# Edge-gated graph layer on one core: other steps for the pieces of rows and lists

## The chip, the core and the metric

One core of a Trainium2 chip runs one launch. The metric is device time in microseconds. The core has a matrix engine (TensorE; PE in the profile, its weight loads PEld), VectorE (DVE), ScalarE (ACT), GpSimd (POOL) and a queue that only issues transfers (SP). ACT and POOL issue transfers too, each in the order of its own program.

## The reference

With B = 16, N = 1024 nodes and D = 256, `adj` has about nine entries other than zero in a column, 24 at most being handled in the main part:

```python
pre_u = einsum('bud,dk->buk', h, W1[:d])
pre_v = einsum('bvd,dk->bvk', h, W1[d:])
hidden = relu(pre_u[:, :, None, :] + pre_v[:, None, :, :] + b1)
S = sigmoid(einsum('buvk,ko->buvo', hidden, W2)[..., 0] + b2[0])
a = einsum('buv,bud->bvd', S * adj, h)
m = einsum('uv,bud->bvd', adj, h) * h
z = beta1 * h + beta2 * (a @ Wa + ba) + beta3 * (m @ Wm + bm)
```

Only edges (u, v) with adj[u, v] other than zero count, so the kernel visits edges and never forms the full `hidden`.

## The kernel before

The batches are four groups g of four, and the nodes v eight tiles vt of 128. A block is one (g, vt); there are 32, in the list `order` (lines 365 to 367): g = 0 and 1 for vt 0 to 5, then vt 6 and 7 of both, then g = 2 and 3. A block has T = 10 steps, each with 128 edges. The main loop (line 684 on) makes 320 steps n, with s = n mod 10, and all engines run their instructions in the order in which the loop writes them: nothing reorders them.

In step n:
- `aggregate(n-1)` (line 560): PE sums the neighbours' rows of the step before, weighted, into `acc`.
- `fetch_val` (line 341) and `fetch(n+4)` (line 453) on POOL: up to two small gathers of edge values, then the gather of 128 rows of `table[g]` into one of five `fetched` buffers, free once it was aggregated.
- `gate(n)`: DVE adds the gathered row to `pc` (line 539) and makes four weighted sums (line 543); ACT makes the sigmoid (546) and the weights `left` (549).
- `left_adj(n+1)` (533), and every fifth step `load_mark` (516), on ACT.
- `do(n)`: DVE work that an earlier step put off.
- `expand(n+2)` (523): PE makes the next `pc`, of which there are two buffers.

A block's own work lies at fixed s. `halves` of the next block (418 to 425) has two PE products at s = 0 and 2, each put in X by ACT and into `low` by DVE one step later (419), and ACT copies at 3, 4 and 6. `turn_over` (578 transposes, 581 ACT copy of LT, 591 DVE `times_h` a step later) stands at s = 1, twice at 7, and at 9. `block_end` (608) stands at s = 3, 4, 5, 6, with DVE's sum into `h_blk` (612) at s = 5 and 7 and the output on SP.

Two kinds of work are cut into pieces and put between, at the end of a step:
- Rows: `rows(k)` makes the left half of a table tile, x W1[:d], in two halves: PE product (384), ACT copy into `tab` (400), and a step after the second half the write to the table on SP (403). `load_hT` on SP (373) brings the transposed x, `copy_h` on ACT's queue (378) copies x itself into the right half of the table. `plan` gives for each tile the step of its load and of its two halves.
- Lists: `lists(vt)` (from line 236) finds the edges of a tile in ten pieces: 1 load of the key on POOL; 2 key (244 DVE, 245 ACT); 3 maxima (251); 4 `cut` and the sorted tops (254 to 266); 5 prefix sums on PE (270); 6 `held` (275 to 285), which reads the PE result; 7 mark (288 to 300, `few` on ACT 298); 8 four transfers of `whose` (304, on ACT's queue for vt from 4), the products of line 307 and the ACT copy `L` (311); 9 indices (315 to 326), which also hands ten value gathers to `fetch_val`, two a step; 10 `onehot` (331). `advance` says in which steps the pieces of lists 4 to 7 stand: an offset each from n = 0, 20, 50 and 80.

`halves`, `rows`, `turn_over`, `block_end` and the PE results of lists from vt = 3 on share the two PSUM buffers `misc`; a new use takes a buffer once its last reader is done.

Before the loop stands an opening, `script`: 16 row halves ("r") for all eight tiles of g = 0, lists 0 to 3 (digits), the first block's `halves` ("h"), list 0's values ("v") and five fetches ("f"). Behind it come `load_mark(0)`, two expands and `left_adj(0)`.

Of the kernel before, what the change touches and what calls it, by code (L numbers as in the profile page):

```python
# [17 lines left out]
def kernel(  # L18
# [44 lines left out]
    NT = N // P  # L63
# [166 lines left out]
    EARLY = 4  # L230
# [200 lines left out]
    def do(step):  # L431
        for f in due.pop(step, ()):
            f()
# [12 lines left out]
    def where(n):  # L446
        k, s = divmod(n, T)
        w, j = divmod(s, TW)
        return k, *order[k], w, j
# [9 lines left out]
    made = [lists(vt) for vt in range(NT)]  # L459
    turn = [(g, vt) for g in range(2) for vt in (*range(FIRST, NT), *range(FIRST))]  # L460
# [8 lines left out]
    for i in range(COPIES):  # L469
        copy_h(turn[i], nc.sync)  # L470

    script = ("r 0 0", "r r 0", "r 1", "0 r 1 1", "0 0 r r", "1 r 0 2 2", "r r 0 0 v 2", "1 1 r r",
              "2 r 1 r", "2 2 r r 1 1 h", "2 h 3 3", "2 2 h 3", "f h h 3", "3 3")
    m = 0
    piece = None
    parts = halves(0)
# [21 lines left out]
            else:  # L498
                next(made[int(c)], None)
    do(len(script) - 100)  # L500

    def scale_late():
        nc.vector.tensor_scalar(ba_b, ba_b, be2, None, ALU.mult)
        nc.vector.scalar_tensor_tensor(bias, bias, be3, ba_b, ALU.mult, ALU.add)
        spread(bias_p, bias)
        nc.vector.tensor_scalar(w_a, w_a, be2, None, ALU.mult)
        nc.vector.tensor_scalar(w_m, w_m, be3, None, ALU.mult)
# [10 lines left out]
    def expand(n):  # L518
        k, g, vt, w, j = where(n)
        pcs[n] = psc.tile([P, GD], FP, name="pc")  # L520
        for h in range(2):
            c = slice(2 * h * D, (2 * h + 2) * D)
            nc.tensor.matmul(pcs[n][:, c], marks[n // TW][:, j * P:(j + 1) * P], cuts[k][:, w, c],  # L523
                             start=True, stop=True)


    def left_adj(n):
        k, g, vt, w, j = where(n)
        i = vt * NW + w
        m = len(QUARTERS[j])  # L530
        o = max(2 * j - 1, 0)
        lefts[n] = wk.tile([P, 2, GB, 2, V], FP, name="left")
        nc.scalar.activation(lefts[n][:, :m, :, 0, :], onehot[:, i, o:o + m, :].unsqueeze(2).to_broadcast([P, m, GB, V]),  # L533
                             AF.Copy, scale=val[:, i, j:j + 1])
# [123 lines left out]

    advance = {0: (3,), 2: (3,), 4: (3,)}
    for i, n in zip(range(EARLY, NT), (0, 20, 50, 80)):  # L660
        for o in (0, 4, 5, 6, 7, 9, 11, 13, 15, 17):
            advance[n + o] = (*advance.get(n + o, ()), i)
    loads, at = {}, {}

    def plan(blocks, ns):

        for k, (load, *pieces) in zip(blocks, ns):
            loads[load] = k
            at.update((n, k) for n in pieces)

    plan(turn[NT:], ((0, 5, 8), (6, 12, 15), (12, 18, 22), (17, 25, 28), (24, 32, 35), (31, 38, 42), (38, 45, 48),
                     (43, 50, 52)))
    plan([(2, vt) for vt in range(NT)], ((62 + 10 * i, 68 + 10 * i, 73 + 10 * i) for i in range(NT)))
    plan([(3, vt) for vt in range(NT)], ((146, 152, 157), (156, 162, 167), *((153 + 10 * i, 158 + 10 * i, 161 + 10 * i)
                                                                             for i in range(2, NT))))
    plan(again, ((103,), (113,), (125,), (133,)))
    begun = set(turn[:NT])
# [2 lines left out]
    for n in range(2):  # L680
        expand(n)
    left_adj(0)
    total = BS * T
    for n in range(total + 2):
        k, s = divmod(n, T)
# [25 lines left out]
        if s == 4 and k < BS:  # L711
            hbs[k] = big.tile([P, GB, D], FP, name="h_blk")
            if k < BS - 1:
                g, vt = order[k]
# [55 lines left out]
    with tc.If(any_left > 0):  # L770
        with ExitStack() as s2:
# [3 lines left out]
            for vt in range(NT):  # L775
# [17 lines left out]
                f = fb.tile([P, 2 * GD], FP, name="fb_f")  # L793
# [83 lines left out]
```

## Time and profile before

| | us |
|---|---|
| median of 4 runs | 1203.81 (1197.35 to 1208.98) |
| the profiled execution | 1200.31 |
| its span, first to last instruction | 1198.5 |
| start of the first line-539 add (step 0) | 68.69 |
| VectorE busy | 1067.3 |
| PE busy, PEld busy | 1100.2, 725.7 |
| ScalarE busy | 841.1 |
| mean granted TensorE clock | 0.966 |

A row of the timeline has the start, the length, the engine, the line, the operation, what it writes and reads, and in brackets how long its engine stood idle before it and what ended that. A row of the table by stretches has the stretch, its length, each engine's busy time with its number of instructions, the granted clock as a share of full speed, the transfers' share and their rate. A row of the waits has the time in all, how often, and the longest.

### The profile page before, as it was taken

Reading aid. Unit: us, or ns where it says so; the run is one execution under the profiler, and the core shown is the slowest. Engines: PE = TensorE matmul, PEld = TensorE weight load, DVE = VectorE, ACT = ScalarE, POOL = GpSimd, SP = SyncE. Lnnn points to the kernel's source line nnn. Section 1 sums busy time; section 2 is a strip of 40 time slices with the busy share of each in tenths; the row PEclk is TensorE's granted clock in tenths of the full one; section 3 lists DMA queues with packets and bytes.
Section 4 is the critical chain, followed back from the end, with each engine's and each line's share of the span. In section 5 each row is a group of like instructions: output and inputs, shape, how many; then the busy total and the mean of one; then the engine's idle time right before and its main releaser. Section 6 shows DMA issues by size and latency. Waiting matters only on the chain. (4 is left out here: it accounts for less than half of the span.)

```text
span 1198.5 us, 23788 instructions
## 1 busy us (share of the span) xinstructions
PE 1100.2 (92%) x7633; PEld 725.7 (61%) x7633; DVE 1067.3 (89%) x3515; ACT 841.1 (70%) x2498; POOL 426.6 (36%) x428
## 2 busy tenths in 40 slices
PE   7667988999899898999999999999999999999986
PEld 6544655666556565666566666666666666666653
DVE  8769879979989987999899999999999999999994
ACT  3346666677667765787677777877877777777873
POOL 1647652433253226323233333333323333333330
PEclk9867999999899999999999999999999999999999
DMA  9996899899979978999999999999999999999992
GB/s 289 293 315 225 285 321 323 315 324 383 318 251 351 364 252 296 372 374 360 353 325 375 376 321 374 368 355 383 366 362 346 350 322 330 329 338 327 336 339 80
DMA packets 147046, 391.39 MB, mean 327 GB/s; under 512 B 16752, under 2 KB 105328, under 8 KB 110704
## 3 DMA queue, kind: packets, MB, share of 16 engines
q0 software_dynamic: 50016, 300.50, 68.0%
q1 hardware_dynamic: 81616, 74.99, 19.5%
q10 hardware_dynamic: 15280, 14.29, 3.7%
q8 instruction: 63, 1.03, 0.3%
q14 instruction: 71, 0.58, 0.1%
HBM read 393.78 MB, written 50.33 MB: 371 GB/s over the span
## 5 line engine op out<-in xcount | busy, mean ns | idle before, releaser
L453 POOL DMA_INDIRECT fetched<-table,uidx x320 | 329.8, 1031 | 677.0 <-PE acc L560 490.3
L543 DVE SCALAR_TENSOR_TENSOR t<-t,w_b 128x256 f32<-128x256 f32 x1280 | 469.7, 423 | 20.1 <-DVE t L539 0.5
L539 DVE TENSOR_TENSOR t<-fetched,pc 128x1024 f32<-128x1024 f32 x320 | 389.2, 1216 | 23.2 <-DMA fetched<-table,uidx 9.7
L560 PE MATMUL acc<-fetched,left 128*32 128x256 f32 x4096 | 331.7, 394 | 29.2 <-ACT left L549 19.4
L549 ACT ACTIVATE left<-left,gt 128x32 f32<-128x32 f32 (+1 forms) x1280 | 299.4, 305 | 10.4
L523 PE MATMUL pc<-X,mark 128*128 128x512 f32 x640 | 238.7, 455 | 19.3 <-DVE t L539 10.6
L560 PEld LDWEIGHTS acc<-fetched,left 128*32 128x32 f32 x4096 | 127.5, 110 | 174.3 <-issue 49.1
L523 PEld LDWEIGHTS pc<-X,mark 128*128 128x128 f32 x640 | 97.6, 192 | 155.2 <-issue 104.5
L546 ACT ACTIVATE gt<-sc,b_b 128x4 f32<-128x4 f32 x320 | 95.4, 298 | 135.0 <-DVE t L543 128.4
L608 PE MATMUL misc<-w_a,LT 128*128 128x256 f32 x496 | 127.3, 379 | 0.0
L608 PE MATMUL misc<-w_m,LT 128*128 128x256 f32 x496 | 127.1, 378 | 0.0
L384 PE MATMUL misc<-w_u,hT 128*128 128x256 f32 x448 | 111.2, 396 | 14.1 <-issue 5.8
L533 ACT ACTIVATE left<-onehot,val 128x128 f32<-128x128 bf16 (+1 forms) x320 | 116.6, 365 | 0.0
L384 PE MATMUL misc<-w_v,hT 128*128 128x256 f32 x448 | 108.7, 386 | 0.0
L543 DVE DVE_READ_ACCUMULATOR t<-t,w_b 128x1 f32 x1280 | 105.3, 82 | 0.0
L384 PEld LDWEIGHTS misc<-w_u,hT 128*128 128x128 f32 x448 | 86.7, 197 | 30.3 <-issue 6.8
L608 PEld LDWEIGHTS misc<-w_m,LT 128*128 128x128 f32 x496 | 93.7, 189 | 17.2
L608 PEld LDWEIGHTS misc<-w_a,LT 128*128 128x128 f32 x496 | 94.2, 190 | 12.8
L568 ACT COPY ev<-acc 128x512 f32<-128x512 f32 x128 | 75.2, 587 | 37.0 <-PE acc L560 29.9
L384 PEld LDWEIGHTS misc<-w_v,hT 128*128 128x128 f32 x448 | 87.3, 195 | 14.6
L341 POOL DMA_INDIRECT val<-in_adjT_dram,vidx x80 | 83.9, 1049 | 33.5 <-issue 20.8
L581 ACT COPY LT<-misc 128x512 f32<-128x512 f32 x128 | 71.1, 576 | 21.5 <-PE misc L578 7.1
(158 smaller groups left out, 834.9 us busy)
## 6 DMA issues: line engine op xcount, KB each, us to landing
h_blk<-in_x_dram SPq DMA_DIRECT2D x31, 512.0 KB
out_dram<-h_blk SPq DMA_DIRECT2D x31, 512.0 KB
hT<-in_xT_dram SPq DMA_DIRECT2D x28, 512.0 KB
table<-tab SPq DMA_DIRECT2D x26, 512.0 KB
table<-in_x_dram ACTq DMA_DIRECT2D x24, 512.0 KB
fetched<-table,uidx POOLq DMA_INDIRECT x320
table<-in_x_dram SPq DMA_DIRECT2D x8, 512.0 KB
table<-fetched SPq DMA_DIRECT2D x6, 512.0 KB
```

The lines of the kernel that those rows point to most:

```text
L341: nc.gpsimd.indirect_dma_start(out=val[:, i, j:j + 1], out_offset=None, in_=adj_flat, in_offset=bass.IndirectOffsetOnAxis(ap=vidx[:, i, j: ...
L384: nc.tensor.matmul(p[:, bb * D:(bb + 1) * D], hT[:, 2 * h + bb, i, :], wt[:, i, :], start=(i == 0 and not begun), stop=(i == DC - 1), skip ...
L453: nc.gpsimd.indirect_dma_start(out=fetched[n % NF], out_offset=None, in_=table[g], in_offset=bass.IndirectOffsetOnAxis(ap=uidx[:, vt * NW ...
L523: nc.tensor.matmul(pcs[n][:, c], marks[n // TW][:, j * P:(j + 1) * P], cuts[k][:, w, c], start=True, stop=True)
L533: nc.scalar.activation(lefts[n][:, :m, :, 0, :], onehot[:, i, o:o + m, :].unsqueeze(2).to_broadcast([P, m, GB, V]), AF.Copy, scale=val[:, ...
L539: nc.vector.tensor_tensor(t, fetched[n % NF][:, :GD].rearrange("p (b d) -> p b d", b=GB), pcs.pop(n).rearrange("p (b d) -> p b d", b=GB), ...
L543: nc.vector.scalar_tensor_tensor(t[:, b, :], t[:, b, :], 0.0, w2_b, ALU.max, ALU.mult, accum_out=sc[:, b:b + 1])
L546: nc.scalar.activation(gt, sc, AF.Sigmoid, bias=b2_b)
L549: nc.scalar.activation(lefts[n][:, :m, b, 1, :], lefts[n][:, :m, b, 0, :], AF.Copy, scale=gt[:, b:b + 1])
L560: nc.tensor.matmul(accs[h][b * 2 * V:(b + 1) * 2 * V, r, :], left[:, i, b].rearrange("p k v -> p (k v)"), f[:, GD + b * D:GD + (b + 1) * D ...
L568: nc.scalar.copy(evs[q], accs.pop(q))
L608: nc.tensor.matmul(pz[:, bb * D:(bb + 1) * D], LTs[k][:, c, 2 * h + bb, i, :], wt[:, c, :], start=False, stop=(i == 1 and c == DC - 1), sk ...
```

## The change

The order and the steps of the pieces change; none is added or taken away, and what is computed is the same.

- In the opening, some row halves go in front of list pieces, and list 3's pieces 6 and 7 move from the script's end to behind the two expands and `left_adj(0)`.
- The row pieces of tiles g = 1 go to s = 7, 8, 9 and 1 (from 0, 2, 5 and 8); those of g = 2 to 8 and 1 (from 8 and 3), and the first two tiles of g = 3 likewise (from 2 and 7), with loads up to 4 steps earlier and one a step later.
- The ten pieces of lists 4 to 7 go to s = 0, 4, 6, 9, 1, 4, 6, 7, 9, 0 (from 0, 4, 5, 6, 7, 9, 1, 3, 5, 7).

```diff
-    script = ("r 0 0", "r r 0", "r 1", "0 r 1 1", "0 0 r r", "1 r 0 2 2", "r r 0 0 v 2", "1 1 r r",
-              "2 r 1 r", "2 2 r r 1 1 h", "2 h 3 3", "2 2 h 3", "f h h 3", "3 3")
+    script = ("r 0 0", "r r 0", "r 1", "0 r 1 1", "0 r r 0", "1 r 0 2 2", "r r 0 0 v 2", "r r 1 1",
+              "2 1 r r", "2 r r 2 1 1 h", "2 h 3 3", "2 2 h 3", "f h h 3")
...
     for i, n in zip(range(EARLY, NT), (0, 20, 50, 80)):
-        for o in (0, 4, 5, 6, 7, 9, 11, 13, 15, 17):
+        for o in (0, 4, 6, 9, 11, 14, 16, 17, 19, 20):
             advance[n + o] = (*advance.get(n + o, ()), i)
...
-    plan(turn[NT:], ((0, 5, 8), (6, 12, 15), (12, 18, 22), (17, 25, 28), (24, 32, 35), (31, 38, 42), (38, 45, 48),
-                     (43, 50, 52)))
-    plan([(2, vt) for vt in range(NT)], ((62 + 10 * i, 68 + 10 * i, 73 + 10 * i) for i in range(NT)))
-    plan([(3, vt) for vt in range(NT)], ((146, 152, 157), (156, 162, 167), *((153 + 10 * i, 158 + 10 * i, 161 + 10 * i)
+    plan(turn[NT:], ((0, 7, 8), (3, 9, 11), (11, 18, 19), (15, 21, 28), (23, 29, 31), (32, 38, 39), (35, 41, 47),
+                     (42, 48, 49)))
+    plan([(2, vt) for vt in range(NT)], ((62 + 10 * i, 68 + 10 * i, 71 + 10 * i) for i in range(NT)))
+    plan([(3, vt) for vt in range(NT)], ((142, 148, 151), (152, 158, 161), *((153 + 10 * i, 158 + 10 * i, 161 + 10 * i)
...
     left_adj(0)
+    for _ in range(2):
+        next(made[EARLY - 1])
```

## The prediction

> **What bounds the kernel now.** I read the page's first two parts, then the busy time by stretches of whole blocks, then VectorE's waits, and then the timeline around each long wait. I count in steps: step n begins at the start of the n-th line-539 add in the timeline, s = n mod 10.
>
> ```profile
> span 1198.5 us, 23788 instructions
> PE 1100.2 (92%) x7633; PEld 725.7 (61%) x7633; DVE 1067.3 (89%) x3515; ACT 841.1 (70%) x2498; POOL 426.6 (36%) x428
> PEclk9867999999899999999999999999999999999999
> ```
>
> DVE is the engine with the least rest (1067.3 of 1198.5 us); PE's 92% counts pipelined matmuls whose weight loads take only 61%.
>
> ```profile
> core 0: us, PE busy (x) PEld busy (x) DVE busy (x) ACT busy (x) POOL busy (x), PEclk, DMA share, GB/s
> 68.70:238.00 169.30, 148.10 (x954) 98.03 (x953) 146.43 (x497) 105.33 (x311) 89.54 (x87) 0.91 0.85 290
> 238.00:274.80 36.80, 34.11 (x237) 22.94 (x235) 30.46 (x97) 26.36 (x80) 14.52 (x15) 0.95 0.93 338
> 274.80:354.10 79.30, 70.87 (x480) 46.32 (x477) 71.16 (x242) 52.79 (x158) 29.79 (x29) 0.94 0.92 322
> 354.10:386.70 32.60, 32.27 (x233) 21.38 (x231) 30.32 (x97) 25.82 (x78) 12.34 (x13) 1.00 0.89 318
> 386.70:469.20 82.50, 72.36 (x474) 47.80 (x478) 71.15 (x242) 53.52 (x159) 29.44 (x29) 0.94 0.88 316
> 469.20:704.50 235.30, 227.86 (x1617) 149.68 (x1608) 212.70 (x675) 178.81 (x538) 74.97 (x73) 0.99 0.97 353
> 736.50:931.30 194.80, 191.25 (x1389) 125.51 (x1388) 181.91 (x576) 153.64 (x462) 62.17 (x61) 1.00 0.98 361
> 931.30:1149.10 217.80, 209.77 (x1515) 133.09 (x1513) 210.89 (x673) 172.07 (x526) 71.77 (x71) 1.00 0.93 334
> ```
>
> The rows are blocks 0-3, 4, 5-6, 7, 8-9, 10-16, 18-23 and 24-30. The last seven have no pieces: 31.1 us each with DVE busy 30.1, the floor. A list adds 71.15 - 2 x 30.12 = 10.9 us of DVE work wherever it stands. What lies above floor plus list work is stall: blocks 0-3 18.9 us (169.3 - 124.4 - 26.0 of lists), block 4 5.7, 5-6 6.2, 7 1.5, 8-9 9.4, 10-16 17.6, together 59.3. Blocks 18-23 already have their row pieces at s = 8 and s = 1, as the change puts the others, and stall 8.2, or 1.37 a block.
>
> ```profile
> DVE low L419 <- ACT X L418: 19.6, 14, 4.6
> DVE h_blk L612 <- PE misc L608: 18.8, 22, 2.7
> DVE LT L591 <- ACT LT L581: 15.8, 11, 3.7
> DVE t L539 <- DMA fetched<-table,uidx: 9.7, 17, 1.5
> DVE made L288 <- PE misc L384: 5.7, 1, 5.7
> ```
>
> DVE waits for PE, straight or through an ACT copy: PE is late, not short of time. Most of the second line is s = 5, where the block's end (PE work at s = 3 to 6) is added to h_blk.
>
> **The change, part by part.**
>
> *Opening.* The timeline there:
>
> ```profile
> 37.76 0.72 ACT L298 CAST few<-made 128x640 uint8<-128x640 f32 x1 [5.98 <-issue]
> 39.02 3.68 PE L384 MATMUL misc<-w_u,hT 128*128 128x256 f32 x8 [3.63 <-issue]
> 45.90 0.55 DVE L288 TENSOR_SCALAR made<-upto,R 128x640 f32<-128x640 f32 x1 [5.69 <-PE misc L384]
> 66.03 0.72 ACT L298 CAST few<-made 128x640 uint8<-128x640 f32 x1 [7.02 <-DVE made L292]
> 68.69 1.22 DVE L539 TENSOR_TENSOR t<-fetched,pc 128x1024 f32<-128x1024 f32 x1 [2.04 <-PE pc L523]
> ```
>
> ACT holds row copies behind `few`, which waits for a list's mark on DVE; PE, with both `misc` buffers uncopied, stands 3.63 us. Behind PE, DVE waits 5.69 us for `made`. After the change the copies go first, but PE's matmul on list 1's mark is now ahead of four row halves and itself waits for that mark (ready at 38.4, PE free at 35.4), so some 2.9 of the 3.63 stay. I take 0.7, and the like gap of 0.85 that PE has at 24.6 for list 0: 1.5, less 0.2 for one copy more behind `few`. The last: list 3's held and mark pieces now stand behind the first expands, so ACT's mark cast and PE's L523 run under DVE's work, and the 2.04 before the first add go. Sum -3.3; bounds -1 (the table's DMAs set the end of the opening) and -5.
>
> *Row pieces.* None is added or removed: eight matmul instructions (1.9 us of PE, an estimate from their 0.21 us spacing and the gaps), one ACT copy (0.59) each. By the weight loads in the timeline, PE's own work in a step is about 1.2 us at s = 8, 1.5 at 1, 1.7 at 9, 2.1 at 7, against 2.7 to 3.1 at 0 and 2 to 6. At s = 3 or 5 a piece made L612 wait:
>
> ```profile
> 373.64 0.75 DVE L612 SCALAR_TENSOR_TENSOR h_blk<-h_blk,be,misc 128x512 f32<-128x512 f32 x1 [1.30 <-PE misc L608]
> 749.03 0.69 DVE L419 TENSOR_TENSOR low<-misc,X 128x512 fp32r<-128x512 f32 x1 [0.45 <-ACT X L418]
> 755.42 0.75 DVE L612 SCALAR_TENSOR_TENSOR h_blk<-h_blk,be,misc 128x512 f32<-128x512 f32 x1 [0.25 <-PE misc L608]
> ```
>
> The first is step 75 (piece at 73); the others are steps 183 and 185 (piece at 181): 1.30 becomes 0.70. Blocks 10-16: 17.6 becomes 7 x 1.37 plus the 3.1 us that step 131 waits for the transposed x of a reloaded block, which nothing here moves: 12.7, so -4.9. Bounds 0 (transfers fill what is freed) and -8. Blocks 4 and 7: the L612 and L591 gaps at 42, 45, 47 and 75 (0.41, 0.55, 1.15, 1.30) go; 41 and 71 pay 0.70 each, and pieces at 48 and 49 give PE 1.2 + 1.7 + 3.0 and 3.8 for the two, 9.7 us in steps 48 to 50 against DVE's 8.9, so step 51's `low` comes an estimated 0.8 late: -3.4 + 1.4 + 0.8 = -1.2. The issues move too. SP's loads of hT come up to 4 steps earlier (one a step later) and its table writes up to 6; table 1's last write is at step 50 instead of 53, its first fetch at 56. ACT's copy issues (0.57) move with the loads, into steps without an ACT queue wait in the rows. I cost these at nothing; if an issue blocks for its lane, up to 1 us each for 10 issues.
>
> *List pieces* (lists 4 to 7). DVE's 10.9 us are unchanged. Removed: L612's waits at 15, 35, 65, 95, two steps behind the L307 matmuls (1.79, 1.89, 0.29, 2.69); L591's at 28, 58, 88, where the L270 result holds one of the two `misc` buffers from s = 7 to DVE's reading at s = 9, so PE and ACT take turns on the other (0.54, 0.91, 0.91); L612's at 25 and 55 (0.38, 0.74). Sum -10.1. Added, first: L270 now at offset 11, read at 14. The buffer is held across s = 1 to 4, where halves and the block's end need two. With a row piece in the same step (11, 31, 91) I follow the chain: low, transposes, LT copy, row, tab copy, halves, X copy; the second `low` comes 1.5 us late; without (61) the held piece's own 1.9 us of DVE hide it. 3 x 1.5 = +4.5. Second: L307 and four ACT DMA issues at s = 7:
>
> ```profile
> 330.34 1.25 ACTq L304 DMA_DIRECT2D whose<-few  x2
> 331.63 0.40 ACT L311 COPY L<-misc 128x290 f32<-128x290 f32 x1 [1.33 <-issue]
> ```
>
> The L copy ended 3.25 us after the sigmoid's start (328.78); the two LT copies (1.2) now queue behind it, and times_h behind them: 4.45 against 3.4 that gate and add cover, +1.1, four times +4.4. Bounds for both: 0 (list work on DVE covers it) and three times as much (below). The fetches of val (two of 1.0 us and 0.3 of issue per step on POOL, five steps) move from steps 16-20, 36-40, 66-70, 96-100 to about four later; POOL's fetches queue behind them as before. I leave the long stalls that stand near them (21, 41, 68, 98: 5.4, 2.9, 3.25, 3.66) as they are. Net -1.2.
>
> **Sum.** -3.3 - 4.9 - 1.2 - 1.2 = -10.6. The profiled execution took 1200.31 us (span 1198.5 and 1.8 around it), 3.5 under the median 1203.81; I take the gain off the median: 1193.2.
>
> **Two rules of the skill, set aside from the sum.** In 414.6 to 418.0 PE was busy 1.81 of 3.40 us at clock 1.00, and from 418.0 to 422.2 the clock was 0.50. The Trainium skill, "TensorE: Matmul & The Clock Gate" (Part 1), has the half clock come after an idle window of some 3.4 us; a half-busy one was enough here. By the rule the slower rival below would cost only its waits and the net would be the sum above; by the row it has its second price. The Trainium skill, "Perfetto Trace Analysis" (Engine Utilization), gives 358 GB/s as a core's share of memory and about 120% of it as the practical ceiling for one core; blocks 10-16 move 353 and 18-23 361. Were 358 a wall, blocks 10-16 could shrink to 235.3 x 353/358 = 232.0 and the -4.9 would be -3.3; the page itself allows more, and so do the 361 of blocks 18-23.
>
> **Rivals.**
>
> *More: -25.8, 1178.* The long stalls near the val fetches (15.2 us together) vanish too, since after the change those five steps follow others without list work. For: all four stand there. Against: their number of fetches and POOL's order stay.
>
> *Almost nothing: 1200.* Transfers are the wall in blocks 7-16 (DMA share 0.97) and the lists only trade waits: -3.3 - 1.2, so 1199.3. For: the fetches wait 9.7 us in all at L539. Against: 18-23 run at 0.98 and 32.5 us a block.
>
> *Slower: 1213.5.* The held `misc` buffer at s = 1 to 4 lets PE idle by half in a clock window, and the half clock falls on the block's end, PE's heaviest stretch. Steps 1 and 3 show such a stretch: granted clock 0.62 and 0.88, and `low` waited 3.38 and 1.32, 4.7 in all. With the 1.5 that is 6.2 a list, four times 24.8 in place of 4.5: -10.6 + 20.3 = +9.7. It decides from 3.8 us a list up (10.6/4 above the 1.1 of the sum). Against: at 58 and 88 the half clock cost under 1 us.
>
> **How the numbers follow.** Forecast 0.50 (1183 to 1201), more 0.15, almost nothing 0.20, slower 0.15. About 1% (12 us) is what a measurement of this kernel tells from no change. Faster by over 1% (under 1191.8): 0.15 and 0.22 of the forecast's 0.50, 0.37; slower: 0.14 of the last; same 0.49. The range 1178 to 1213 leaves out half of "more" and half of "slower". The forecast's own range is 1183 to 1201.
>
> **What would show it.** The first L539 add at 65 us, with no wait for pc; L612's waits at s = 5 under 0.4 us in blocks 10-16, 0.5 for L419 at s = 3 there; blocks 10-16 near 32.5 us. Wrong: L419 or L591 waits over 2 us at steps 13, 33, 93 or 18, 38, 68, 98; half clock there; or L539 waiting for fetched at most steps.

## The result and the profile after

The changed kernel takes 1207.36 us (median of 50 runs) against 1203.37 (76 runs beside it): a ratio of 1.0034, interval [1.0022, 1.0047]. It is slower by some 4 us, inside the 1% that the prediction called "same", and on the other side of the forecast of 1193.2. A second comparison (e6 below, beside a kernel before of 1182.10 us) gave 1.0035 [1.0016, 1.0054]. The profiled execution of the changed kernel took 1214.42 us, 7 over its median, so its sums lie high; places and single waits are read from it, and sizes from the ratios of the experiments and from e6, a second trace of the same kernel.

The file has one blank line less: line 539 of before is 538 after, 591 is 590, 612 is 611, 608 is 607, 560 is 559, 581 is 580, 578 is 577, 523 is 522. Lines up to 500 stay.

Busy time by stretches of blocks after, in the columns of before (blocks 0-3, 4, 7 and 10-16):

```profile
66.67:245.68 179.01, 146.79 (x942) 96.07 (x946) 144.84 (x495) 107.33 (x314) 85.02 (x84) 0.87 0.83 287
245.68:285.13 39.45, 35.97 (x235) 23.75 (x228) 30.94 (x99) 25.64 (x77) 20.44 (x20) 0.96 0.84 286
...
364.42:399.55 35.13, 32.73 (x232) 21.14 (x230) 30.85 (x100) 24.20 (x73) 20.75 (x21) 1.00 0.87 304
...
480.30:714.15 233.85, 224.22 (x1619) 146.79 (x1617) 212.83 (x679) 177.86 (x534) 83.58 (x82) 0.99 0.99 361
```

DVE's busy time (the third engine) is nearly the same. Blocks 0 to 3 take 179.0 where they took 169.3; blocks 4 and 7 take 2.6 and 2.5 more; blocks 10 to 16 take 1.5 less (block 10 alone 3.6 more, blocks 11 to 16 5.1 less). The fifth engine, POOL, is busy for 20.4 and 20.8 us in blocks 4 and 7, where it was 14.5 and 12.3: the fetches of val now fall there, and in block 10. The code of blocks 18 to 30 is unchanged, and they take 5.2 us more than before in this execution; in e6 they do not (blocks 18 to 23: 198.9 here, 194.5 in e6, 194.8 before).

VectorE's waits after, in the view of waits (total, times, longest):

```profile
DVE low L419 <- ACT X L418: 34.1, 23, 5.1
DVE LT L590 <- ACT LT L580: 22.0, 8, 5.3
...
DVE h_blk L611 <- PE misc L607: 9.6, 16, 2.6
```

The wait of the block's end was halved (18.8 to 9.6), as the pieces' new steps should do. In its place `low` waits 14.5 us more and `times_h` (LT) 6.2 more. Both were named as what would show the prediction wrong, and both stand where it said. At steps 13, 33 and 93 `low` waits 5.11, 4.21 and 4.19 us (2.48, 4.19 and 5.45 in e6); at 18, 38, 68 and 98 `times_h` waits 2.45, 2.91, 2.24 and 2.50 (2.14, 2.56, 2.17 and 2.02 in e6). Another 8.1 us of the LT line stand at steps 8 and 12 (2.79 and 5.27); e6 has no such waits there. The first add came at 66.67 us, not at 65, without its old wait for `pc`.

The timeline of the changed kernel from step 91 to 93, where L270 of list 7 and a row product share step 91:

```profile
441.75 0.94 PE L270 MATMUL misc<-R,sums 128*128 128x1 f32 x8
442.11 0.69 DVE L419 TENSOR_TENSOR low<-misc,X 128x512 fp32r<-128x512 f32 x1
...
444.95 3.32 PE L384 MATMUL misc<-w_u,hT 128*128 128x256 f32 x8 [1.44 <-ACT LT L580]
...
452.24 0.59 ACT L418 CAST X<-misc 128x512 fp32r<-128x512 f32 x1 [1.87 <-PE misc L384]
452.86 0.69 DVE L419 TENSOR_TENSOR low<-misc,X 128x512 fp32r<-128x512 f32 x1 [4.19 <-ACT X L418]
```

L270's result keeps one `misc` buffer, so everything else goes through the other in turn: `low` reads it, PE transposes into it, ACT copies LT, PE makes the row product, ACT copies `tab`, PE makes the second half. From one `low` to the next are 10.75 us. The row product waits 1.44 us for its buffer and then takes 3.32 us for eight matmuls, which take 1.99 in the same step of e9 below. From 442.0 to 444.9 PE was busy 1.35 of 2.90 us, and the granted clock from 444.9 to 452.0 is 0.76. The rule of the Trainium skill that the prediction weighed ("TensorE: Matmul & The Clock Gate", Part 1: the half clock comes after an idle window of some 3.4 us) would have no half clock here, where PE's longest pause was 1.44 us; the row decides, as it did there. A half-busy stretch does not always bring it either: in e9 PE was busy 1.75 of the 3.40 us up to 421.2, and the clock from there to 427.5 was 1.00.

The other place, steps 97 and 98 of the changed kernel:

```profile
469.27 0.51 ACTq L304 DMA_DIRECT2D whose<-few  x1
...
470.47 2.02 ACTq L304 DMA_DIRECT2D whose<-few  x2
472.54 0.40 ACT L311 COPY L<-misc 128x290 f32<-128x290 f32 x1 [2.03 <-issue]
472.99 1.12 PE L577 MATMUL misc<-ident,ev 128*128 128x128 f32 x4 [2.73 <-ACT L L311]
...
474.76 0.69 DVE L590 TENSOR_TENSOR LT<-LT,hT 128x512 f32<-128x512 f32 x1 [2.50 <-ACT LT L580]
```

ACT spends 3.1 us on four issues (0.51, 0.61 and 2.02 for two), with short activations among them, before it copies `L`. The copy frees the `misc` buffer that PE's second transposes need: PE stands 2.73 us, and DVE 2.50 behind PE and ACT.

### The profile page after: what moved, and what is told of

The parts are those of the page before. It is cut to its first block, busy times and chain, and to the rows that moved or that the text cites. A ratio compares the mean times of both kernels' runs of the same rounds, so it can differ in the third digit from the quotient of the medians.

```text
span 1212.5 us, 23801 instructions
## 1 busy us (share of the span) xinstructions
PE 1098.8 (91%) x7633; PEld 721.0 (59%) x7633; DVE 1065.5 (88%) x3515; ACT 840.8 (69%) x2498; POOL 427.7 (35%) x428
## 5 line engine op out<-in xcount | busy, mean ns | idle before, releaser
L559 PE MATMUL acc<-fetched,left 128*32 128x256 f32 x4096 | 323.2, 394 | 25.6 <-ACT left L548 13.2
L559 PEld LDWEIGHTS acc<-fetched,left 128*32 128x32 f32 x4096 | 122.6, 110 | 171.4 <-issue 55.2
L567 ACT COPY ev<-acc 128x512 f32<-128x512 f32 x128 | 75.1, 587 | 45.8 <-PE acc L559 35.4
L577 PE MATMUL misc<-ident,ev 128*128 128x128 f32 x512 | 75.9, 280 | 15.6 <-ACT L L311 10.5
```

What stands on the lines that cost most here:

```text
L559: nc.tensor.matmul(accs[h][b * 2 * V:(b + 1) * 2 * V, r, :], left[:, i, b].rearrange("p k v -> p (k v)"), f[:, GD + b * D:GD + (b + 1) * D ...
L577: nc.tensor.transpose(pt[:, i * P:(i + 1) * P], ev[:, r, c * P:(c + 1) * P], ident)
```

## The experiments

Sixteen kernels in four groups (e1 to e4, e5 to e8, e9 to e12, e13 to e16); each group ran on one chip beside the kernel before, whose median there was 1183.34, 1182.10, 1199.64 and 1203.51 us. Ratios are to that, so a comparison between groups is one of ratios and not of times.

| kernel | ratio | interval |
|---|---|---|
| e1 opening alone | 0.9964 | [0.9947, 0.998] |
| e2 rows alone | 1.0073 | [1.0049, 1.0096] |
| e3 lists alone | 1.0091 | [1.0065, 1.0118] |
| e4 opening and rows | 1.0042 | [1.0022, 1.0063] |
| e5 the same, loads a step ahead | 0.9976 | [0.9952, 0.9999] |
| e6 the changed kernel again | 1.0035 | [1.0016, 1.0054] |
| e7 changed, mark written by SP | 0.9919 | [0.9894, 0.9944] |
| e8 e7, L270 moved, loads ahead | 0.9866 | [0.9834, 0.9898] |
| e9 e7, L270 moved | 0.982 | [0.9784, 0.9855] |
| e10 before, mark written by SP | 0.9965 | [0.994, 0.9991] |
| e11 opening, mended lists, old rows | 0.9868 | [0.9839, 0.9898] |
| e12 e5, mark written by SP | 0.9967 | [0.9943, 0.9991] |
| e13 opening, later rows, loads ahead | 0.9931 | [0.9902, 0.996] |
| e14 opening, early rows | 1.0018 | [0.9994, 1.0042] |
| e15 e8 again | 0.9843 | [0.9807, 0.988] |
| e16 e9 again | 0.9865 | [0.9827, 0.9902] |

### The parts alone: e1 to e4

e1 is before with the new opening:

```diff
-              "2 r 1 r", "2 2 r r 1 1 h", "2 h 3 3", "2 2 h 3", "f h h 3", "3 3")
+              "2 1 r r", "2 r r 2 1 1 h", "2 h 3 3", "2 2 h 3", "f h h 3")
...
+    for _ in range(2):
+        next(made[EARLY - 1])
```

> The kernel before with the new opening alone. Theory (the lists' new offsets eat what the opening and the rows gain): the first line-539 add comes at 66 to 67 us instead of 68.7 and the rest is as before, so -2 us, ratio 0.998. Rival (the opening's gain is given back in the first block, where the transfers of table 1 and the value fetches of lists 1 to 3 wait): 1.000.

Measured 0.9964: 4.3 us less. Its first add starts at 65.14. The step was right.

e2 is before with the new row plans:

```diff
-    plan([(2, vt) for vt in range(NT)], ((62 + 10 * i, 68 + 10 * i, 73 + 10 * i) for i in range(NT)))
+    plan([(2, vt) for vt in range(NT)], ((62 + 10 * i, 68 + 10 * i, 71 + 10 * i) for i in range(NT)))
```

(and the new tables of the tiles of g = 1 and 3).

> The kernel before with the new steps of the row pieces alone, lists and opening as before. Theory (lists eat it): -4 to -6 us, ratio 0.996; in blocks 10-16 the waits of L612 at s = 5 are 0.25 us instead of about 1.3, and those of L419 at s = 3 are 0.45. Rival (earlier loads and table writes crowd the transfers): 1.000 to 1.004, with more waits of L539 for fetched.

Measured 1.0073: 8.6 us more, though the waits of L612 at s = 5 went almost whole (1.1 us left in steps 0 to 99). The forecast of this part has the wrong sign. The row product of step 108 waits 6.76 us for its load here, and block 11 takes 39.6 us where e1 takes 32.7.

e3 is before with the new list offsets:

```diff
-        for o in (0, 4, 5, 6, 7, 9, 11, 13, 15, 17):
+        for o in (0, 4, 6, 9, 11, 14, 16, 17, 19, 20):
```

> The kernel before with the new offsets of lists 4 to 7 alone. Theory (lists eat it): at s = 8 of steps 18, 38, 68, 98 times_h waits 2.2 to 2.9 us each, as in the changed kernel's trace; the waits of 4 to 5 us at s = 3 need a row piece in the step of L270 and come only where the old row plan has one there (it has none at 11, 31, 61, 91), so under 1 us. Removed waits 10 us, added 10 to 12: ratio 1.000 to 1.002. Rival (holding the misc buffer over s = 1 to 4 is enough by itself): 4 us more at each of 13, 33, 63, 93, ratio 1.010 or more.

Measured 1.0091. Two things stand in its trace. L591 waits 2.86, 3.00, 2.61 and 2.83 us at 18, 38, 68 and 98, as in the whole change. But `low` waits under 0.5 us at 13, 33, 63 and 93: L270's result is held across s = 1 to 4 here too, and without a row product in the same step that costs nothing (the granted clock in steps 91 to 93 is 1.00). The four waits at L591, 11.3 us together, are about the size of the loss of 10.8. And L612 still waits 2.00, 1.99 and 1.95 at 15, 35 and 95, which the new list steps were to remove; the rows alone (e2) remove them. They belong to the row pieces, not to the products of L307. (At step 15 there is one exception: e14 has no row piece there and waits 2.44 us; why is open.)

e4 has the diffs of e1 and e2 together.

> The changed kernel with the lists' old offsets (opening and rows new). Theory (lists eat it): -6 to -8 us against the kernel before, ratio 0.994, and so 10 to 12 us under the changed kernel. Rival (the parts do not add, since the rows' new steps collide with old list pieces as well: rows at s = 7 and 9 with L270 at s = 7 and its reading at 9): 0.998 to 1.002.

Measured 1.0042, what the two parts add to (-0.36 and +0.73%). Its trace holds the reason for the rows' loss. SP's queue at step 102, then the row product of step 108 and DVE's next add:

```profile
459.72 0.34 SPq L403 DMA_DIRECT2D table<-tab  x1
460.15 0.39 SPq L373 DMA_DIRECT2D hT<-in_xT_dram  x1
460.59 1.49 SPq L373 DMA_DIRECT2D hT__5233<-in_xT_dram  x1
462.18 20.01 SPq L717 DMA_DIRECT2D h_blk<-in_x_dram  x1
...
486.41 3.75 PE L384 MATMUL misc<-w_u,hT 128*128 128x256 f32 x8 [6.30 <-DMA hT<-in_xT_dram]
492.42 1.22 DVE L539 TENSOR_TENSOR t<-fetched,pc 128x1024 f32<-128x1024 f32 x1 [6.36 <-PE pc L523]
```

The load of hT (line 373) stands behind the table write of the row before it (403). In e1, with the old plan, the same load goes out at 443.04, early in step 98 (442.87 to 446.17), since the table write comes later in SP's program. With the new plan the write is put off to step 62+10i, the very step of the load, and the loop runs what was put off first. So the load goes out at step 102 together with two others, lands 26.1 us later, and PE stands 6.30 us for it. Block 11 takes 39.8 us, against 32.7 in e1. The rest of the loss is early: blocks 0 to 5 take 240.6 us, against 236.1 in e1.

### The row loads ahead of the table write: e5, and the changed kernel again: e6

```diff
-    plan([(2, vt) for vt in range(NT)], ((62 + 10 * i, 68 + 10 * i, 71 + 10 * i) for i in range(NT)))
+    plan([(2, vt) for vt in range(NT)], ((61 + 10 * i, 68 + 10 * i, 71 + 10 * i) for i in range(NT)))
```

(on e4; also the loads of 32, 142 and 152 one step earlier).

> The opening and the row plans of the change, the lists left as before (the kernel that gave 1.0042), but each row load of blocks 62 to 162 (and the one at 32) planned one step earlier, so that it stands on SP's queue ahead of the table write of the row before it (the write is queued at steps 62+10i, as the load was). In the kernel before, the load of step 102 went out at step 98 (459.5 us) for a product at 499.7; with the new plans it went out at 102 (460.2) for a product asked for at 480, landed 26.1 us later, and PE stood 6.3 us (DVE 6.4). Theory A (the late load is what the rows lose): the waits on the hT transfer vanish, the load of step 101 goes out near step 98, and the ratio is 0.988 to 0.995. Theory B (the loss is the place of the products on PE, beside the lists' and the halves' work at steps 1 and 8): the ratio stays at 1.001 to 1.006 though the transfer waits are gone.

Measured 0.9976, 0.66% under e4 (about 8 us); e4 ran on another chip with the same time of before. SP's queue in e5:

```profile
443.89 0.47 SPq L373 DMA_DIRECT2D hT<-in_xT_dram  x1
458.82 0.34 SPq L403 DMA_DIRECT2D table<-tab  x1
```

The load goes out at step 98 again and lands after 5.4 us; no row product of blocks 7 to 16 waits for its load, and block 11 takes 32.0 us. Theory A holds for the transfer, but the ratio is above its range: the rows still bring nothing against the opening alone.

e6 is the changed kernel without an edit.

> The changed kernel once more, beside the others on their chip. If the parts simply add (0.9964, 1.0073 and 1.0091): 1.012 to 1.014. If lists and rows take each other's waits away, as the removed waits at steps 15, 35 and 95 say (they went with the rows alone, and stayed with the lists alone): 1.002 to 1.007, as in the first comparison (1.0034).

Measured 1.0035, where the three parts add to 1.0128: lists and rows overlap. In the changed kernel too the load goes out at step 102, behind the table write, but no row product of blocks 7 to 16 waits for its load in either of its traces, and block 11 takes 32.5 and 32.1 us. So the cost that e2 and e4 pay there, some 7 us, is not paid in the changed kernel. The issue of L716 beside it holds SP for 6.89 and 9.04 us, where in e4 the same one (L717) held it for 20.01, and block 10, in which the product stands, runs longer than in e4 (37.4 and 35.4 us against 32.6); why the transfers are quicker there was not shown. What else overlaps was not told apart.

### The list's mark off ACT's queue: e7 and e10

```diff
-                (nc.gpsimd if vt < EARLY else nc.scalar).dma_start(whose
+                (nc.gpsimd if vt < EARLY else nc.sync).dma_start(whose
```

> The changed kernel with one edit: the four writes of a list's mark (to whose) are issued by SP and not by ACT. Theory C (at s=7 the copy of L and so PE's next transposes stand behind four issues on ACT, 0.5 to 1 us each): the waits of L590 at steps 18, 38, 68, 98 (2.2 to 2.9 us each) fall under 0.9 us, and the time falls by 6 to 10 us against the changed kernel (ratio lower by 0.005 to 0.008). Rival (PE at half clock and the extra products of L307 make the wait, the issues only stand beside it): the waits stay over 1.8 us each and the time changes by under 2 us.

Measured 0.9919, 1.16% under e6 on the same chip (14 us). Step 97 and 98 of e7:

```profile
436.66 2.51 SPq L304 DMA_DIRECT2D whose<-few  x4
440.16 0.38 ACT L311 COPY L<-misc 128x290 f32<-128x290 f32 x1
442.36 0.69 DVE L590 TENSOR_TENSOR LT<-LT,hT 128x512 f32<-128x512 f32 x1 [0.35 <-ACT LT L580]
```

The issues are on SP's queue, `L` is copied without a wait, and `times_h` waits 0.35 us. In steps 0 to 99 the LT waits fall from 8.9 to 0.7 us, and the stretch from 393.75 to 381.61 us, with DVE busy for 347.4 and 347.3 of it. Theory C holds, and its size was too small. The Trainium skill, "Trainium Kernel Development and Optimization" (Quick Reference, Key Constraints), says that spreading transfers over the issuing engines saves only the issue time; the trace agrees, and that time, 3.1 us a list, is what was in the way here.

e10 makes the same edit in the kernel before.

> The kernel before with one edit: the list's mark written by SP and not by ACT (its issues stood at s=3, ahead of L612 at steps 15, 35, 65, 95). If four issues on ACT cost the step in which they stand wherever it is: ratio 0.993 to 0.997 and the waits at 15, 35 and 95 (1.8 to 3.1 us) under 1.3 us. If they cost only at s=7, where PE and DVE wait for ACT's copy next: 0.999 to 1.001 and those waits stay.

Measured 0.9965 [0.994, 0.9991]: 4 us. The waits at 15, 35 and 95 stay (3.10, 1.89, 2.01), so the place of the gain is not settled. By the medians the same edit is worth three times as much in the changed kernel (on another chip), where the issues stand at s = 7.

### L270 out of the row's step: e8 and e9

e9 is e7 with one more edit, e8 has the loads ahead as well:

```diff
-        for o in (0, 4, 6, 9, 11, 14, 16, 17, 19, 20):
+        for o in (0, 4, 6, 7, 9, 10, 16, 17, 19, 20):
```

The new offsets move three pieces: L270 from 11 to 9, `cut` before it from 9 to 7, and `held` after it from 14 to 10.

> The changed kernel with three edits: the list's mark written by SP, the row loads planned one step earlier, and L270 of a list moved from offset 11 to 9 (its buffer given back at 10), so that it no longer shares steps 11, 31 and 91 with a row product. If the theories A and C hold and the waits of 4.2 to 5.1 us at steps 13, 33 and 93 come from the shared step: those waits fall under 1 us, and the ratio is 0.982 to 0.990, below every kernel so far. If the shared step is not the cause: L419 still waits over 3 us at 13, 33, 93, and the ratio is 0.991 to 0.998.

> The changed kernel with two edits: the list's mark written by SP (that gave 0.9919), and L270 of a list at offset 9 with its buffer given back at 10; the row loads stand as in the change. Theory D (the shared step of L270 and a row product makes the waits at 13, 33, 93, which were 4.12, 4.17 and 2.50 us with the mark on SP; no product waited on its load there): the waits fall under 1 us, and the ratio is 0.985 to 0.988, all that the third edit brought together with the loads (0.9866). Rival (the earlier loads brought half of that last step): 0.989 to 0.992.

Measured 0.9866 for e8, 7 us under e7 on the same chip, and 0.982 for e9, a little below what Theory D expected. Step 91 to 93 in e9:

```profile
420.54 0.69 DVE L419 TENSOR_TENSOR low<-misc,X 128x512 fp32r<-128x512 f32 x1
421.28 1.99 PE L384 MATMUL misc<-w_u,hT 128*128 128x256 f32 x8 [1.02 <-DVE low L419]
...
427.55 0.69 DVE L419 TENSOR_TENSOR low<-misc,X 128x512 fp32r<-128x512 f32 x1 [0.45 <-ACT X L418]
```

The same row product stands in the same step. With both buffers free for it, from `low` to `low` are 7.01 us instead of 10.75, and the wait is 0.45 us. At 13, 33 and 93 `low` waits 0.46, 0.46 and 0.45 in e9 and 0.37, 0.46 and 0.46 in e8. Theory D holds, with two limits. L270 of lists 4 and 5 now stands beside the row products of steps 9 and 29; its buffer is held for one step there and not for three, so what costs is the shared step together with the long hold, not the shared step alone. And block 1 is not free of stalls: `low` waits 2.96 us at step 11 in e9, and at 11 and 13 it waits 3.36 and 1.98 in e15, 3.53 and 2.14 in e16. In e8 it does not, and the cause is open.

### What rows and lists are worth: e11 to e14

e11 is e1 with the mended lists (mark on SP, L270 at offset 9), e12 is e5 with the mark on SP; their edits are those above.

> The new opening and the mended lists (mark on SP, L270 at offset 9) with the row plans of before. The rows' worth, once nothing else is in their way: the row plans of the change remove some 19 us of waits of L612 at s=5, and gave back 7 us as waits of L419 at s=1 and 1 to 4 us as waits on fetched. If that net of 6 to 10 us holds: 0.992 to 0.996. If the opening with rows (0.9976 with their loads ahead) against the opening alone (0.9964) tells it, the rows are worth nothing: 0.985 to 0.989, as with them (0.9866).

> The new opening, the row plans of the change with their loads ahead, the lists at the steps of before with their mark written by SP. If the lists' new steps are worth something once mended: 0.993 to 0.997 here, against 0.9866 with them. If all that the mended lists brought is the mark on SP: 0.986 to 0.989.

On one chip: 0.9868 (old rows), 0.9967 (old lists), 0.982 for e9 with both new. So the lists' new steps, once mended, are worth about 1.5%; e12 also has the loads ahead, which e9 has not, and against e15, which has them (0.9843, on another chip), it is 1.2%. The rows' worth beside them, 0.5% by these two medians, is not certain: the intervals of e9 and e11 overlap, and e9 again (e16) gave 0.9865.

e13 and e14 split the row plans at step 61, on e1:

```diff
-    plan([(2, vt) for vt in range(NT)], ((62 + 10 * i, 68 + 10 * i, 73 + 10 * i) for i in range(NT)))
+    plan([(2, vt) for vt in range(NT)], ((61 + 10 * i, 68 + 10 * i, 71 + 10 * i) for i in range(NT)))
```

(e13, with the first two of g = 3; e14 has the new table of steps 0 to 52 instead, with the load of 32 at 31).

> The new opening with the change's row plans for the blocks from step 61 on alone (loads one step ahead), the plan of steps 0 to 52 and the lists as before. By blocks of the profiled executions, these rows with their loads ahead took 375.8 us for blocks 6 to 16 against 380.7 with the old plans: 4.9 us. If that is their worth: 0.992 (0.990 to 0.994). If the loads ahead only undo a loss and the places of the products bring nothing: 0.996 to 0.998, as the opening alone.

> The new opening with the change's row plan of steps 0 to 52 alone (the load of step 32 one ahead), the later rows and the lists as before. By blocks of the profiled executions, this plan took 238.9 us for blocks 0 to 5 against 236.1: the waits of L612 at 15, 35, 45, 55 go, and waits of L419 at 11, 31, 51 (1.2, 1.3, 3.2) and on fetched at 21, 23, 43 (1.0, 1.9, 1.8) come. If that is so: 0.998 to 1.001, a loss against the opening alone (0.9964). Rival (the removed waits outweigh the new ones): 0.990 to 0.995.

Measured 0.9931 and 1.0018 against 0.9964 for the opening alone: by these ratios the later rows gain about 4 us when their loads are ahead, and the early rows lose about 6. e1 ran in another group, and the intervals of e13 and e1 overlap, so the gain is not certain; e13 against e14, on one chip, is clear. In e14, blocks 0 to 5 took 254.6 us against 249.9 in e13: blocks 0 to 3 9.6 more, where `low` waits at steps 11, 13, 21, 23 and 31 (1.18, 1.70, 4.91, 1.95, 1.86; in e13 only 4.45 at 21), and block 4 7.0 less. In the first group e4's blocks 0 to 5 took 4.5 us more than e1's. So the loss of some 5 us stands in both.

### The two best on one chip: e15 and e16

> The kernel with all three edits (0.9866 on its chip), beside the one without the loads ahead (0.982 on another) on one chip. If the earlier loads are worth something once the lists are mended too: 0.002 to 0.006 below the other. If they matter only where a load of some 26 us stands behind a fast block: within 0.002 of it.

> The kernel with the mark on SP and L270 at offset 9, the loads as in the change, on the same chip as the one with the loads ahead. If the difference between 0.982 and 0.9866 was the chip's (the chip with the longer times has waits of 2 to 5 us at steps 18, 21, 38, 68 and 98 in the kernel before, which this kernel does not have): the ratio follows the chip, 0.980 to 0.984 where before takes about 1200 us, 0.985 to 0.990 where it takes about 1183.

Measured 0.9843 and 0.9865: 0.0022 apart with intervals of 0.007, so whether the loads matter once the lists are mended stays open. The ratio of e9 did not follow the time of the kernel before either (0.982 at 1199.64, 0.9865 at 1203.51). In their four runs both are faster than the kernel before, by 1.3 to 1.8%, and so than the changed kernel.

## Why the prediction was wrong

*Opening, -3.3: right.* 4.3 us measured (e1), inside its bounds. The wait for `pc` before the first add went; part of the gap came back as a wait of `low`, 4.2 us in the changed kernel's opening against 0.95.

*Rows in blocks 10 to 16, -4.9, and 4 and 7, -1.2: the mechanism right, the sum incomplete.* From block 11 on the waits at s = 5 are 0.25 us and `low` at s = 3 waits 0.45, as written; blocks 11 to 16 took 196.4 us where they took 201.5, the size forecast. Block 10 took 37.4 against 33.8. It now has fetches of val of list 7, and with the new lists alone it is longer too (35.7 in e3, 33.7 in e1), as are blocks 4 and 7 (35.9 and 35.1 against 34.4 and 33.0). The sum moved these fetches at no cost; how much of this other blocks gave back was not told apart. One gap is that the rows of steps 0 to 52 were costed only where they touch blocks 4 and 7: over blocks 0 to 5 they lose some 5 us (e4 against e1, e14 against e13). The other is "SP's loads of hT come up to 4 steps earlier (one a step later) and its table writes up to 6 ... I cost these at nothing". The two moves were counted, but not their order: the write moved in front of the load on SP, and loads planned for the same step 62+10i went out four steps later. In e2 and e4 this costs some 7 us in block 11; in the changed kernel itself it cost nothing that the traces show.

*Lists, -1.2: the failed step is the size of both added terms, and with it the owner of the removed one.* L270 beside a row product: 1.5 us each expected, 5.11, 4.21 and 4.19 in the profile. The chain that I followed was the right one, but I gave each link its usual length; with PE idle by half before it and a lower clock, the row product took 3.32 us instead of about 2.0. L307 with four issues: 1.1 us each expected, 2.24 to 2.91 measured. I followed only ACT's queue; PE's second transposes also wait, for the buffer that the late copy of `L` frees. The two added terms are 23.6 us in the profile, and 21.0 in e6, where the sum had 8.9. That most of the loss is theirs is shown by taking them away: the mark on SP gives 14 us (e7), and L270 at offset 9 with the loads ahead another 7 (e8), and the kernel is then faster than forecast. Of the removed 10.1, the 6.4 at 15, 35 and 95 belong to the row pieces (e2 and e3).

*The slower rival* named the place of one stall and an idle PE, but not its price. It wanted 6.2 us a list, and 3.8 to decide by itself; measured were 13.5 us in all, 3.4 a list, so it took the L307 term as well to make the kernel slower. Its cause, the held buffer by itself, is refuted by e3 and by step 63, where a list piece stands without a row product and `low` does not wait. The lower clock did come, but on the row product (0.58 from 444.95 to 448.3) and not on the block's end. *Almost nothing* (transfers are the wall): moving the mark, L270 and the loads (e6 to e8, on one chip) gave 1.7% with the same transfers, so transfers were not the wall that held the changed kernel. *More* came in part: the stalls of 5.4 and 2.9 at steps 21 and 41 are 1.65 and 2.11, but at 68 and 98 the lists' own waits stand in the place of the old ones.

*The forecast's range.* 1207.36 lies inside 1178 to 1213, but the forecast of a gain had the sign wrong because the two list terms were taken far below the top of their bounds, three times as much: at 13.5 and 10.1 us the same sum gives -10.6 + 14.7 = +4.1, close to the +4.0 measured (with e6's 12.1 and 8.9 it is +1.5). That closeness is partly luck, since the rows' term left out the early blocks and the removed waits were in part not the lists'.

## What to carry to other kernels

When a piece is moved in a hand-ordered program, list for each queue what now stands in front of what: a load planned for the same step went out four steps later, because a table write had moved ahead of it. Two pieces that are each harmless in a step can share a small pool of buffers there, and then the chain through the one buffer left is what counts; look for the buffers' holders before the engines' busy time. Transfers issued from a compute engine's queue belong where nothing waits for that engine's next instruction, or on a queue that only issues.

## What the runs showed of the hardware

- A 512 KB load of hT landed 5.4 us after its issue in e5, and 26.1 us when it went out beside two other loads in e4. The issue of the third of these (L717) then held SP for 20.01 us; in e5, with the loads apart, it took 2.74.
- The same kernel before took 1182 to 1183 us in two of the groups and 1200 to 1204 in the two others. The record gives the first and the last group the same chip number (10; 1183.34 and 1203.51 us), so this is not shown to be a property of the chip. Where it took longer, there are waits of L591 near the val fetches (e10: 1.83, 2.30 and 3.06 us at steps 18, 68 and 98), and in the kernel before ACT stands idle for 4.37 us at step 98; in e1, where before took 1183, there is no wait above 0.7 us at steps 18, 38, 68 and 98. What releases ACT there is none of the core's own instructions by the trace, and its cause stays open. It does not explain the result, since the ratio of the changed kernel was the same beside both (1.0034 and 1.0035).
